# Attention in a fused transformer block: the last batch's additional maxima spread over steps, the first biases written into later steps, and the first batches' halves in another ring

## The chip, the cores and the metric

The kernel runs on one core of a Trainium2 chip. The metric is the device time of one execution in microseconds (us). Matrix products run on TensorE (PE), with its weight loads shown as a row of their own (PEld); reductions and elementwise work run on VectorE (DVE), ScalarE (ACT) and GpSimd (POOL). Most transfers are issued from the queue of SyncE (SP).

## The reference, cut to what matters

The whole block is attention, a routed feed-forward, a gated linear attention with its own feed-forward, and the routed feed-forward again. Only the first part is touched by the change:

```python
q = split_heads(x @ Wq + bq)                 # x is layer-normed, 8 batches of 512 x 256
k = split_heads(x @ Wk + bk)                 # 16 heads of 16
v = split_heads(x @ Wv + bv)
scores = einsum('bhqd,bhkd->bhqk', q, k) * scale
sparsity = scores.max(axis=-1) - scores.mean(axis=-1)
_, top_idx = top_k(sparsity, U)              # U = 307 of 512 queries
...                                          # those queries get softmax(scores) @ v, the others 0
out = out.transpose(0, 2, 1, 3).reshape(b, l, D)
return out @ Wo + bo
```

So each score is needed twice: once for the row maxima, which choose the queries, and once for the exponentials. The kernel subtracts the mean of the keys first, so that a row's mean is zero, and computes the outputs of all queries; those that are not chosen are multiplied by zero at the end.

## The kernel before, in words

The attention stage walks over 128 steps, `steps = (b, m, e, k)`: eight batches, two chunks of eight heads (`m`), two interleaved sets of four heads (`e`), four tiles of 128 positions (`k`). One loop over `n` does two things in each round. For the step `ahead` it makes four row maxima, one for each head `j` (`max_one`): two products on a strip of 32 rows (L582), with the high and the low halves of the queries, and a DVE reduction (L588). For the step `here`, 16 rounds behind (`LAG`), it makes four exponentials (`exp_one`): three products (L608) and an ACT activation (L615). In a round the eight items go in two groups, each of two exponentials and two maxima, and `together` interleaves their products, so that four heads' products stand side by side in four strips of the array. After each group PE multiplies the exponentials of the round before with the values (`weigh`, L630).

PSUM banks: exponentials take one of three banks of `bank`; maxima take one of the four of `bank_m`, which also holds the projections of the fronts and the transposed maxima (`mxT_ps`). A bank comes free when DVE or ACT has read it.

The fronts. `front(b, ...)` makes a batch's queries, keys and values in small pieces. In a round of the first 14 (`FIRST`) the pieces of batches 0 and 1 are drawn from `pieces`; later fronts run one piece a round, from round 21 (`LEAD`) on, for the batch two ahead. `halves` splits a projection into a high half (ACT, L446) and a low one (ACT at L452 and a POOL subtraction at L453; for the very first chunk a DVE operation at L448). Both lie in tiles of the tag `half`, a ring of four, until DMAs have moved them into `qh`, `ql` and `km` (L391). The tag `e` is a ring of ten for the exponentials and, earlier, for the scratch tile of `sum_stats`.

`place_maxima` runs some rounds after a group of maxima is complete (the list `full` has the round): POOL copies the maxima into `apart` (L548), PE transposes them (L554), ACT writes the two tiles `top` (L558, L562), also of the tag `half`, a DMA puts the whole ones into `neg` (L561), and POOL or, for the last batch, DVE makes `tops` (L566, L570 and L571), which the exponentials read as a third operand. When the last maxima are placed, `top_queries` runs 26 rounds of `max` and `match_replace` on DVE (L659, L662) over `neg`; `weights_of` then makes the weights (L147, L148), and `weigh_outputs` starts the end of the stage (L161, L164).

The additional maxima. From round 112 on, each fourth round also makes the maxima of one more step, all four at once, after the round's two groups:

```python
all_maxima(ahead)
if n >= 112 and n % 4 == 0 and coming < len(steps):
    ahead = steps[coming]
    together([max_one(*ahead, i, bank_m) for i in range(4)])
    all_maxima(ahead)
```

This happens in rounds 112, 116 and 120, and the last maxima are done in round 124, not 127.

`add_bias(b)` adds the output bias to a batch of the residual `xres` on POOL (L398); it is called for batches 0 to 2 in round 11.

The tile framework orders the instructions of each engine when the program is built, by priority and by when it reckons that operands are ready; the text's order is followed mostly, not always. Buffers of a tag are waited for by semaphores.

## Time and profile before

| | us |
|---|---|
| median of 3 runs | 1603.43 |
| lowest, highest | 1598.21, 1610.94 |
| profiled execution, its time | 1599.7 |
| its span, first to last instruction | 1598.0 |
| mean granted TensorE clock in it | 0.98 |

Busy time and its share of the span: PE 1547.5 us (97%), weight loads 860.5 (54%), DVE 943.9 (59%), ACT 704.5 (44%), POOL 454.5 (28%). The attention stage is the first third: step 16's exponentials begin at 71.7 us, step 112's at 443.6, step 143's end at 551.1, and the weights of the outputs are done at 552.6. Matmuls are pipelined and their ends are modelled, so that a busy PE need not be a fast one. A row of the timeline is: start, duration, engine, line, operation, output and input, shapes, number, and in brackets how long the engine had been idle and what ended that.

### The profile page before, as it was taken

The page shows a single profiled execution, that of the slowest core. Times are in us where ns is not written, and L with a number is a line of the kernel's source. Part 1 is how long each engine was busy: PE and PEld are TensorE (multiplying, and loading weights), DVE is VectorE, ACT ScalarE, POOL GpSimd, SP SyncE. Part 2 cuts the span into 40 slices and gives each one's busy share as a digit, 9 for nine tenths or more (in the row PEclk, how much of TensorE's full clock was granted, in tenths as well). Part 3 has the DMA queues.
Part 4 walks back from the last instruction along what each step waited for, and adds up shares of the span by engine and source line. Part 5 has one row for each costly group of instructions (what it writes and reads, how often), then busy time and mean ns, then how long its engine had stood idle before and what let it go on. Part 6 is the DMA issues. An engine that isn't in the chain of part 4 may idle for free.

```text
span 1598.0 us, 21558 instructions
## 1 busy us (share of the span) xinstructions
PE 1547.5 (97%) x7982; PEld 860.5 (54%) x7982; DVE 943.9 (59%) x1974; ACT 704.5 (44%) x1290; POOL 454.5 (28%) x547
## 2 busy tenths in 40 slices
PE   6799999999999999999999999999999999999999
PEld 3344444444444376655564556546545655767666
DVE  6688776776776974547744566467275532354332
ACT  4377777677765843442255225432631542221110
POOL 4653453452220241123433233234243210000000
PEclk9899999999996999999999999999999999999999
DMA  5301112112110051100000001000000010011100
GB/s 188 122 16 68 42 42 81 42 42 81 42 42 2 3 171 27 40 2 13 1 0 0 0 2 27 0 0 1 1 1 1 0 28 1 23 31 40 40 27 27
DMA packets 38553, 52.65 MB, mean 33 GB/s; under 512 B 9068, under 2 KB 22580, under 8 KB 38448
## 3 DMA queue, kind: packets, MB, share of 16 engines
q1 hardware_dynamic: 37648, 50.09, 9.6%
q8 instruction: 63, 1.03, 0.3%
q10 hardware_dynamic: 800, 1.18, 0.2%
q14 instruction: 42, 0.34, 0.1%
HBM read 21.24 MB, written 4.33 MB: 16 GB/s over the span
## 4 chain that ended last, share of the span: by engine, by line
PE 78%; DVE 11%; ACT 4%; POOL 4%; issue 2%; DMA 2%; SPq 0%; ACTq 0%; POOLq 0%; DVEq 0%
PE y_ps L1087 17%; PE h_ps L1113 11%; PE s L608 10%; PE av L630 8%; PE swi_ps L1140 8%; PE proj_ps L1226 7%; PE s L582 5%; DVE pr L1259 2%; PE v_ps L505 2%; DVE pr L1249 2%; PE gla_y L1356 2%; PE q_ps L435 2%; PE k_ps L435 2%; POOL o L1276 1%; PE chT_ps L944 1%
## 5 line engine op out<-in xcount | busy, mean ns | idle before, releaser
L588 DVE TENSOR_REDUCE mx<-s 128x1 f32<-128x512 f32 x512 | 325.8, 684 | 119.2 <-PE s L582 118.1
L615 ACT ACTIVATE e<-s 128x512 f32<-128x512 f32 x512 | 276.0, 600 | 127.5 <-PE s L608 121.1
L1087 PE MATMUL y_ps<-w,h 128*128 128x256 f32 x1024 | 236.6, 387 | 8.2 <-DVE h L1122 7.6
L1113 PE MATMUL h_ps<-xnT,w 128*128 128x512 f32 x512 | 228.2, 594 | 0.0
L1087 PEld LDWEIGHTS y_ps<-w,h 128*128 128x128 f32 x1024 | 194.8, 193 | 48.8 <-DVE h L1122 13.2
L1113 PEld LDWEIGHTS h_ps<-xnT,w 128*128 128x128 f32 x512 | 94.7, 190 | 105.8 <-issue 103.8
L630 PE MATMUL av<-e,va 128*32 128x512 f32 (+1 forms) x1216 | 148.7, 559 | 2.1 <-ACT st L640 2.0
L582 PE MATMUL s<-km,qh 32*128 32x512 f32 x512 | 137.5, 508 | 8.5 <-DMA km<-half 4.4
L1121 ACT ACTIVATE h<-h_ps,b 128x512 f32<-128x512 f32 x96 | 65.3, 685 | 176.7 <-PE h_ps L1113 176.7
L1122 DVE TENSOR_TENSOR h<-h,mk 128x512 f32<-128x512 f32 x128 | 94.1, 749 | 82.7 <-ACT h L1121 62.0
L608 PE MATMUL s<-qh,km 32*128 32x512 f32 x512 | 139.4, 508 | 0.9 <-ACT e L615 0.8
L1098 DVE TENSOR_TENSOR xres<-xres,y_ps 128x512 f32<-128x512 f32 x47 | 32.2, 685 | 155.1 <-PE y_ps L1087 117.9
L1140 PE MATMUL swi_ps<-zT,w_up 128*128 128x512 f32 x256 | 122.4, 597 | 0.3 <-DVE h L1149 0.3
L1140 PE MATMUL swi_ps<-zT,w_gate 128*128 128x512 f32 x256 | 121.6, 593 | 0.0
L1087 PE MATMUL y_ps<-w_down,h 128*128 128x256 f32 x512 | 117.5, 380 | 0.0
L1226 PE MATMUL proj_ps<-q_w,rT 128*128 128x512 f32 x256 | 115.3, 594 | 0.5 <-ACT al L1209 0.4
L608 PE MATMUL s<-ql,km 32*128 32x512 f32 x512 | 112.9, 408 | 0.0
L608 PE MATMUL s<-tops,takes 4*128 4x512 f32 x512 | 110.3, 402 | 0.0
L582 PE MATMUL s<-km,ql 32*128 32x512 f32 x512 | 110.2, 412 | 0.0
L582 PEld LDWEIGHTS s<-km,qh 32*128 32x128 f32 x512 | 55.5, 187 | 101.5 <-DVE mx L588 68.4
L1087 PEld LDWEIGHTS y_ps<-w_down,h 128*128 128x128 f32 x512 | 95.1, 190 | 19.0 <-issue 7.4
L1146 ACT ACTIVATE h<-swi_ps 128x512 f32<-128x512 f32 x64 | 38.1, 595 | 139.9 <-PE swi_ps L1140 139.7
(235 smaller groups left out, 2186.9 us busy)
## 6 DMA issues: line engine op xcount, KB each, us to landing
mk<-md SPq DMA_DIRECT2D x32, 256.0 KB
qh<-half SPq DMA_DIRECT2D x63, 128.0 KB
ql<-half SPq DMA_DIRECT2D x63, 128.0 KB
km<-half SPq DMA_DIRECT2D x63, 128.0 KB
out<-xres SPq DMA_DIRECT2D x15, 256.0 KB
xres<-in_L_attn_a_x SPq DMA_DIRECT2D x7, 512.0 KB
w<-in_f_w1T SPq DMA_DIRECT2D x1, 1024.0 KB
w<-in_f_w2T SPq DMA_DIRECT2D x1, 1024.0 KB
```

The source lines that it names most:

```text
L435: nc.tensor.matmul(ps, w[:, c, bass.ts(m, P)], x[:, c, :], start=(c == 0), stop=(c == NC2 - 1),)
L582: nc.tensor.matmul(s, (qh, ql)[i].bitcast(HALF)[rows, e, bass.ts(k, P)], km.bitcast(HALF)[rows, e, :], start=(i == 0), stop=(i == 1),)
L588: nc.vector.tensor_reduce(mx[:, b % 2, m, e, r : r + 1], s, AX.X, ALU.max)
L608: nc.tensor.matmul(s, keys.bitcast(HALF), queries.bitcast(HALF), start=(i == 0), stop=(i == 2),)
L615: nc.scalar.activation(ex, s, AF.Exp, scale=1.0 / DH**0.5)
L630: nc.tensor.matmul(av[32 * j : 32 * j + 32, queries], va[:, 8 * kt + 4 * m + j, DH * e : DH * e + 2 * DH], es[j][:, queries], start=(kt == ...
L1087: nc.tensor.matmul(y[0][:, bass.ts(i, D)], h[f][:, bass.ts(2 * u + i, P)], w[:, f, :], start=(f == 0), stop=(f == NF - 1),)
L1113: nc.tensor.matmul(ps, w1[:, c, bass.ts(f, P)], xT[g][:, c, :], start=(c == 0), stop=(c == NC2 - 1),)
L1121: nc.scalar.activation(hf, ps, AF.Relu, bias=b1[:, f : f + 1])
L1122: nc.vector.tensor_tensor(hf, hf, mk[g][:, f, :], ALU.mult)
L1140: nc.tensor.matmul(ps, w[:, c, bass.ts(f, P)], zT[g][:, c, :], start=(c == 0), stop=(c == NC2 - 1),)
L1226: nc.tensor.matmul(ps, rT[b // G4][:, c, bass.ts(b % G4, P)], q_w[:, c, m], start=(c == 0), stop=(c == NC2 - 1),)
```

## The change

It does three things.

1. The additional maxima of the last batch are no longer made four at once in rounds 112, 116 and 120. They are put into a list, `extra`, and made one a round, and two a round from 120 on, after the round's groups. The books (`all_maxima`) are kept as before, in the same rounds; the placing of batch 7's maxima of chunk 0 goes one round later.
2. `add_bias` for batches 0, 1 and 2 is called in rounds 18, 22 and 26, not three times in round 11.
3. The halves of batches 0 and 1 and the first pair of `top` tiles are taken from the ring `e` of ten, not from the ring `half` of four.

```diff
+            def half_tile(first, name):
+
+                tag, bufs = ("e", 10) if first else ("half", 4)
+                return a2.tile([P, L], F32, tag=tag, name=name, bufs=bufs)
+
@@ halves
-                    hi, lo = (
-                        a2.tile([P, L], F32, tag="half", name=f"half{b}", bufs=4)
-                        for i in range(2)
-                    )
+                    hi, lo = (half_tile(alone, f"half{b}") for i in range(2))
@@ place_maxima
-                whole, hi = (
-                    a2.tile([P, L], F32, tag="half", name=f"top{b}", bufs=4) for i in range(2)
-                )
+                whole, hi = (half_tile(b + m == 0, f"top{b}") for i in range(2))
@@ all_maxima
             coming = 0
+            extra = []
...
-                    full.append((n + 2, (b, m, (0, 1))))
+                    full.append((n + 2 + b // (NB - 1), (b, m, (0, 1))))
@@ the loop
-                    all_maxima(ahead)
-                    if n >= 112 and n % 4 == 0 and coming < len(steps):
-                        ahead = steps[coming]
-                        together([max_one(*ahead, i, bank_m) for i in range(4)])
+                    if n >= 112 and n % 4 == 0 and coming + 1 < len(steps):
+                        extra = [(*steps[coming + 1], i) for i in range(4)]
                         all_maxima(ahead)
+                        all_maxima(steps[coming])
+                    else:
+                        all_maxima(ahead)
+
+                    for _ in range(2 if n >= 120 else 1):
+                        if extra:
+                            together([max_one(*extra.pop(0), bank_m)])
...
-                    if n == 11:
-                        for b in range(3):
-                            add_bias(b)
...
+                    if n in (18, 22, 26):
+                        add_bias((n - 18) // 4)
```

In the built program DVE, ACT and SP keep their order but for the placing of batch 7's first maxima (a few places later); PE's order changes from round 112 on. On POOL, the first `tops` come between the normalizing operations of batch 2, the low half of batch 1's last keys comes ahead of the bias additions, and these, written into rounds 18 to 26, stand in POOL's order around the values' biases of batch 1: two before the first pair, one before the second, and all three ahead of the `apart` copy of round 17.

## The prediction

> **What bounds the kernel now.** I read the page first: TensorE (PE) is busy 97% of the span, so time is lost where PE stands still or where its clock is cut. The slices show both places (slices of 40 us; the third row is the granted clock).

> ```profile
> PE 1547.5 (97%) x7982; PEld 860.5 (54%) x7982; DVE 943.9 (59%) x1974; ACT 704.5 (44%) x1290; POOL 454.5 (28%) x547
> ...
> PE   6799999999999999999999999999999999999999
> ...
> PEclk9899999999996999999999999999999999999999
> ```

> The first two slices are thinly filled, and slice 13 (480 to 520 us) has six tenths of the clock. Both are in the attention stage, the first 553 us, which the change touches. Next I read the table of stages. A step's edges are the starts of its first exponential (L615, four to a step). Columns: PE, weight loads, DVE, ACT, POOL busy, clock, DMA.

> ```profile
> 381.46:385.62 4.16, 4.16 (x34) 1.49 (x37) 2.99 (x5) 3.84 (x8) 0.51 (x1) 1.00 0.01 4
> ...
> 443.59:449.87 6.28, 5.60 (x42) 2.11 (x45) 5.14 (x9) 4.00 (x8) 2.12 (x3) 1.00 0.00 1
> ...
> 477.14:483.22 6.08, 5.32 (x45) 2.26 (x44) 5.48 (x10) 2.65 (x5) 0.77 (x1) 0.94 0.01 3
> ...
> 495.44:500.63 5.19, 5.19 (x40) 2.08 (x44) 2.58 (x5) 2.17 (x4) 0.20 (x1) 0.50 0.00 0
> ```

> Step 96 takes 4.16 us; step 112, with the same pieces of a front and a burst of four additional maxima, takes 6.28 and leaves PE idle for 0.68. Step 120, the third burst, takes 6.08, idles 0.76, and the clock falls in it. Step 123 runs wholly at half clock: 5.19 where step 100, equal in work, takes 3.08. The timeline shows what PE waits for in a burst: a free bank, that is, a DVE reduction (L588).

> ```profile
> 465.42 0.18 PEld L582 LDWEIGHTS s<-km,qh 32*128 32x128 f32 x1 [0.99 <-DVE mx L588]
> 465.42 0.50 PE L582 MATMUL s<-km,qh 32*128 32x512 f32 x1 [0.55 <-DVE mx L588]
> ```

> Then the end of the stage: DVE starts the top-k rounds at 508.27, when the last row of maxima has landed, and is busy without a break until the weights at 551.93; the last exponentials end at 551.1. The two chains are level, and DVE's is the last.

> ```profile
> 508.27 0.43 DVE L656 COPY work<-neg 128x512 f32<-128x512 f32 x1 [1.23 <-DMA neg<-top]
> ...
> 547.85 3.35 DVE L147 RECIPROCAL neg<-den 128x512 f32<-128x512 f32 x1
> ...
> 551.93 0.69 DVE L148 SCALAR_TENSOR_TENSOR nrm<-work,neg 128x512 f32<-128x512 f32 x1
> ```

> Last, the timeline of the start. The halves of batch 1's second chunk (ACT L446) wait 5.77 us for POOL's `tops`, since all share four buffers; PE starts no matmul between 55.2 and 60.13; and POOL holds three bias adds (6.98 us) ahead of the next half and of the `apart` copy that step 17's transposes need.

> ```profile
> 57.52 1.26 POOL L571 TENSOR_TENSOR tops<-top,top 128x512 fp32r<-128x512 f32 x1
> ...
> 58.81 0.69 ACT L446 ACTIVATE half<-q_ps,bq 128x512 fp32r<-128x512 f32 x1 [5.77 <-POOL tops L571]
> ...
> 61.95 6.98 POOL L398 TENSOR_TENSOR xres<-xres,bo 128x1024 f32<-128x1024 f32 x3
> ...
> 73.14 0.21 POOL L548 COPY apart<-mx 128x32 f32<-128x32 f32 x1 [0.23 <-DVE mx L588]
> ```

> **The clock, as this trace has it.** Half-clock stretches last 6.8 us (59.2 to 66.1), 6.8 (72.9 to 79.7) and 30.7 (482.5 to 513.2), all multiples of 3.41. I weighed each matmul record by columns, by its share of 128 rows and of 128 columns, and doubled those of plain f32 (`av`, `q_ps`, `v_ps`, ...), which follow each other at twice the distance of the halves'. In the 3.41 us before each fall the sum is 0 to 2048; no stretch of 3072 or more is followed by one; it returned to full after 3072 to 3136 and more, while 1600 to 3104 left it at half. So about 3000 in 3.41 us is the level. A full step weighs 1088 (exps) + 1024 (maxima) + 2048 (`av`) = 4160.

> **Part 1, the late maxima.** Same instructions, other places: twelve maxima go from three bursts (steps 112, 116, 120) to lone ones, one a step in 112 to 119 and two in 120 and 121. The placing of the last batch's first maxima goes from step 119 to 120; its `tops` are first read in step 128, eight steps later, so this costs nothing.
> - Removed. Without bursts, at full clock, steps 112 to 123 would take what the same places took elsewhere: 4.16 + 4.09 + 4.17 + 3.09 + 3.09 (steps 96, 97, 50, 99, 100), then 3.1 each for seven and 0.6 more for two with transposes (step 119's 3.77): 41.5. The trace has 443.59 to 500.63 = 57.0. So 15.5 goes: some 8 in bursts, 7.4 at half clock.
> - Added. A lone maximum has two products in one row group that follow each other. Four together take 0.34 (first product) + 0.23 (second); a lone one takes as long, less what the next group, on other rows, runs beside its second product. Bounds: 0.23 (the first alone shows) and 0.7 (a whole group's share, weights and all); I take 0.5, nearer to the group. Twelve make 6.0 (2.8 to 8.4). DVE does five reductions in 3.0 us of a 3.6 us step and six in 3.6 of 4.1: it keeps up.
> - Step 124 to the top-k start: 7.64 at half clock, some 6.5 at full: 1.1 saved.
> - Does the clock hold? A step with one lone maximum weighs 4416 in 3.6 us, which is 4180 in 3.41; with two, 4672 in 4.1 us, 3890. Both are over 3000.
> [...] No run here shows a lone one yet.
> Sum: 15.5 - 6.0 + 1.1 = 10.6 earlier for DVE's top-k chain, which then carries the end alone, 43.5 us from its start. The exps (19 steps at 2.2 from step 125) now end some 4 us ahead of it, so PE stands for 4 us before the `nrm_ps` products (L161). That is below the level, so the clock falls there and the products of L161 and L174 run partly at half: 0 to 5, I take 2.5.

> **Parts 2 and 3, the start.** The halves of batches 0 and 1 and the first tops get the exps' ring of ten, which nobody uses before step 16. ACT's wait of 5.77 goes, and so does an earlier one: the tops at 51.14 and 52.45 held a bank that PE waited 1.07 for. Then step 13's maxima, at 65.10 now (DVE idle 6.58), come at about 57.5, right behind step 12's, and all follows 7.6 earlier. But POOL: in the built program the three adds, though written in steps 18, 22 and 26, still stand ahead of step 17's `apart`; only the key half (L453) now goes before them. From 53.71 to that copy POOL has 2.18 + 1.57 + 1.26 + 1.26 + 0.21 + 1.26 + 0.42 + 6.98 + 2.79 = 17.9 and gaps: `apart` at 71.8. PE would be there by 70.9; it did the transposes at 78.48. So 6.6 is gained there, not 7.6. Behind the transposes in PE's queue stand the second group of step 17 and all later exps, so the whole chain waits. The `tops` of step 16's exps are ready by 57.6, and the ring's buffers of batch 1's second chunk, whose key transfers were issued at 65.2 to 72.6 before and come earlier now, are needed by step 18 only: no cost.
> Then the clock. Steps 14 and 15 are maxima alone, 1024 in 2.5 us, so it falls there as before, and the wait for POOL keeps it low. A window at half costs 3.41 x (1 - 3.08/5.19) = 1.4. Before, it returned at 79.72 on 3088, a near thing. I take two windows beyond step 17: -2.8, giving 3.8. Bounds: 7.6 (no cap by POOL, no window) and -4.6 (eight windows, till batch 2's dense front pieces, which start in step 21, lift the sum).

> **Sum** against the profiled execution (1599.7, span 1598.0, 1.7 around it): 10.6 - 2.5 + 3.8 = 11.9, so 1587.8. This execution is 3.7 below the median, 1603.43, and 1.5 above the lowest; I give the number as it stands. Faster by over 1% means below 1587.4; 1% is about what a measurement of this kernel can tell from no change.

> **Rivals.**
> - A: the clock comes back at once in step 17 and PE's stand before L161 costs nothing: 1599.7 - 10.6 - 6.6 = 1582.5. For it: the return at 79.7 after two windows. Against it: nine windows at half from 482.5 with PE busy for 30.39 of 30.70. [...]
> - B: the late half clock comes all the same, from the two-a-step steps: 15.5 - 7.4 - 6.0 = 2.1, with PE not ahead at the end, and 3.8: 1593.8. For it: that stage is where it fell. Against: 3890 is well over the level.
> - C, slower: the half clock of steps 14 to 17 holds on. Each bare step costs 5.19 - 3.08 = 2.1 more. The 14.7 of the other gains is used up from seven such steps; held through step 37, twenty steps, it costs 42: 1627. For it: full steps gave 2592 to 3104 and did not end it late; against: no front pieces there, and from step 21 each adds to the sum.
> - D: the change does not do what it says: adds still ahead, lone maxima at 0.7, the exps' ring held up by a late DMA: 1600.

> **How the numbers follow.** Forecast 0.50 (its own range 1581 to 1595, half of it below 1587.4), A 0.20, B 0.13, C 0.09, D 0.08. Faster 0.25 + 0.20 + 0.02 from B = 0.47; slower 0.08, C but for its shorter forms; same 0.45. The range: A with the cheapest lone maxima (3.2 less) and some of POOL's cap gone is 1578; up to D and the short forms of C, 1602.

> **What would show it.** Right: no step of 6 us at 112, 116, 120; no half clock from 482 on; the top-k copy (L656) some 14 us earlier; PE idle just before L161; ACT's L446 without a wait for `tops`; step 13's reductions right behind step 12's; PE waiting for `apart` in step 17. Wrong: steps 112 to 121 as long as before, a half-clock stretch over three windows after step 17, or L656 less than 8 us earlier.

## The result, and the profile after

The changed kernel took 1588.57 us in the median of 6 executions (1585.32 to 1594.44), beside 1605.2 of the kernel before: a ratio of 0.990 [0.986, 0.994]. Twelve more executions in a later measurement gave 1594.51 (1587.21 to 1599.63) beside 1603.83, a ratio of 0.994 [0.991, 0.997]; the median of all 18 is 1590.0. Ratios, here and below, leave out the four executions that took over 1.5% more than the fastest of their kernel (three of before, one of part 2 alone); medians do not. The forecast was 1587.8. The profiled execution took 1585.32 (span 1583.6), 14.4 less than the profiled one of before.

First the page of the changed kernel: the engines, then TensorE's 40 slices and the granted clock. The 6 that the clock had in slice 13 is gone; an 8 now stands in slice 14, at the hand-over from the exps to the outputs.

```profile
PE 1536.1 (97%) x7982; PEld 858.6 (54%) x7982; DVE 942.4 (60%) x1974; ACT 703.6 (44%) x1290; POOL 454.0 (29%) x547
...
PE   6899999999999899999899999999999999999999
...
PEclk9899999999999899999999999999999999999999
```

**The late steps.** The table by stage of the changed kernel, steps 112, 120 and 124 (columns: window, length, busy time and count of PE, PEld, DVE, ACT and POOL, granted clock, DMA share, GB/s):

```profile
440.78:445.15 4.37, 4.37 (x36) 1.68 (x39) 3.60 (x6) 3.88 (x8) 0.71 (x1) 1.00 0.01 2
...
471.30:476.51 5.21, 4.81 (x48) 2.22 (x44) 4.19 (x8) 3.63 (x8) 0.21 (x1) 1.00 0.02 6
...
487.40:492.87 5.47, 4.54 (x47) 2.21 (x50) 3.25 (x6) 3.96 (x10) 1.09 (x3) 1.00 0.02 6
```

Step 112 is 4.37 long where it was 6.28, PE is never idle in it, and the clock is 1.00 throughout; the half clock of 30.7 us from 482.5 is not there. From step 112 to step 124 it is 46.62 us where it was 57.04. Step 120, though, is 5.21 with 0.40 of PE idle, and step 124 has 0.93.

The timelines of the top-k chain and of the hand-over behind it, DVE and then PE:

```profile
494.04 0.43 DVE L656 COPY work<-neg 128x512 f32<-128x512 f32 x1 [1.24 <-DMA neg<-top]
...
537.71 0.69 DVE L148 SCALAR_TENSOR_TENSOR nrm<-work,neg 128x512 f32<-128x512 f32 x1
...
538.45 4.92 PE L161 MATMUL nrm_ps<-nrm,spread 32*128 32x512 f32 x16 [3.29 <-DVE nrm L148]
543.30 6.35 PE L174 MATMUL ao_ps<-wo_a,outC 128*128 128x256 f32 x16
```

The chain starts 14.2 us earlier (508.27 before), and `nrm` as much. PE now stands 3.29 us before L161, the clock falls at 538.4 for 10.2 us, and the products of L161 take 4.92 where they took 3.03, those of L174 6.35 where they took 3.72. The first addition of `ao` to the residual (POOL, L181) is 10.7 earlier, not 14.2. The 3.5 lost here came back in later stages, which drew less half clock in this execution: from `nrm` to the end it is 1046.1 before and 1045.9 after.

**The start.** Lines of the timeline up to step 17, after the change (line numbers are those of the changed kernel: what was L446 is L448 here, L398 is L403, L548 is L550, L554 is L556):

```profile
51.70 0.69 ACT L448 ACTIVATE half<-q_ps,bq 128x512 fp32r<-128x512 f32 x1 [1.12 <-PE q_ps L440]
...
53.37 14.54 DVE L588 TENSOR_REDUCE mx<-s 128x1 f32<-128x512 f32 x24
...
62.58 4.66 POOL L403 TENSOR_TENSOR xres<-xres,bo 128x1024 f32<-128x1024 f32 x2
...
68.57 2.36 POOL L403 TENSOR_TENSOR xres<-xres,bo 128x1024 f32<-128x1024 f32 x1
...
72.23 0.22 POOL L550 COPY apart<-mx 128x32 f32<-128x32 f32 x1
...
72.50 1.12 PE L556 MATMUL mxT_ps<-ident,apart 128*128 128x128 f32 x4 [1.40 <-POOL apart L550]
```

ACT's halves wait for their projection and no longer for `tops`; DVE makes 24 reductions in a row where it stood 6.58 us; step 16 starts at 64.20 instead of 71.74. The three adds (L403) are still ahead of `apart`, and PE waits for it. Step 17 takes 8.39 us, at half clock (64.0 to 81.1), and step 20 starts at 85.20 instead of 88.43: of 7.5 us, 3.2 are left.

### The profile page after: what moved, and what is told of

Same layout as the page of the kernel before. It is cut to its first block, busy times and chain, and to the rows that moved or that the text cites. A ratio compares the mean times of both kernels' runs of the same rounds, so it can differ in the third digit from the quotient of the medians.

```text
span 1583.6 us, 21546 instructions
## 1 busy us (share of the span) xinstructions
PE 1536.1 (97%) x7982; PEld 858.6 (54%) x7982; DVE 942.4 (60%) x1974; ACT 703.6 (44%) x1290; POOL 454.0 (29%) x547
## 4 chain that ended last, share of the span: by engine, by line
PE 74%; DVE 11%; POOL 5%; ACT 4%; issue 3%; DMA 2%; SPq 0%; POOLq 0%; DVEq 0%; ACTq 0%
PE y_ps L1092 16%; PE h_ps L1118 10%; PE s L608 9%; PE swi_ps L1145 8%; PE av L630 7%; PE proj_ps L1231 7%; PE s L582 4%; DVE pr L1264 2%; PE q_ps L440 2%; POOL o L1281 2%; DVE pr L1254 2%; PE k_ps L440 2%; PE gla_y L1361 2%; PE v_ps L507 2%; DVE w L1256 2%
## 5 line engine op out<-in xcount | busy, mean ns | idle before, releaser
L588 DVE TENSOR_REDUCE mx<-s 128x1 f32<-128x512 f32 x512 | 325.3, 684 | 108.8 <-PE s L582 107.7
L615 ACT ACTIVATE e<-s 128x512 f32<-128x512 f32 x512 | 275.9, 600 | 119.5 <-PE s L608 115.0
L1092 PE MATMUL y_ps<-w,h 128*128 128x256 f32 x1024 | 232.9, 383 | 8.7 <-DVE h L1127 8.1
L630 PE MATMUL av<-e,va 128*32 128x512 f32 (+1 forms) x1216 | 144.4, 543 | 2.0 <-ACT st L640 2.0
L582 PE MATMUL s<-km,qh 32*128 32x512 f32 x512 | 135.6, 501 | 5.8 <-DMA km<-half 4.1
L582 PE MATMUL s<-km,ql 32*128 32x512 f32 x512 | 109.5, 404 | 0.0
L582 PEld LDWEIGHTS s<-km,qh 32*128 32x128 f32 x512 | 54.4, 184 | 96.1 <-DVE mx L588 64.4
```

The source lines that it names most:

```text
L582: nc.tensor.matmul(s, (qh, ql)[i].bitcast(HALF)[rows, e, bass.ts(k, P)], km.bitcast(HALF)[rows, e, :], start=(i == 0), stop=(i == 1),)
L588: nc.vector.tensor_reduce(mx[:, b % 2, m, e, r : r + 1], s, AX.X, ALU.max)
L615: nc.scalar.activation(ex, s, AF.Exp, scale=1.0 / DH**0.5)
L630: nc.tensor.matmul(av[32 * j : 32 * j + 32, queries], va[:, 8 * kt + 4 * m + j, DH * e : DH * e + 2 * DH], es[j][:, queries], start=(kt == ...
L1092: nc.tensor.matmul(y[0][:, bass.ts(i, D)], h[f][:, bass.ts(2 * u + i, P)], w[:, f, :], start=(f == 0), stop=(f == NF - 1),)
```

## How far single executions differ, and why

So each kernel can be split into what it costs at equal half-clock time and how much of that time it draws (+- is one standard error):

| kernel | executions | median us | half clock, mean us | at equal half clock, against before |
|---|---|---|---|---|
| before | 56 | 1603.64 | 72.2 +- 2.6 | 0 |
| changed | 18 | 1590.0 | 61.1 +- 2.6 | -7.4 +- 0.5 |
| part 1 alone | 10 | 1595.31 | 55.8 +- 2.7 | -2.8 +- 0.7 |
| part 3 alone | 10 | 1603.83 | 84.6 +- 5.7 | -4.2 +- 0.7 |
| part 2 alone | 10 | 1603.75 | 71.2 +- 6.0 | +0.7 +- 0.7 |
| parts 2 and 3 | 10 | 1603.05 | 83.9 +- 4.1 | -4.7 +- 0.7 |
| late fillers | 10 | 1607.09 | 70.4 +- 3.6 | +5.6 +- 0.7 |
| changed, bias fetched later | 10 | 1591.01 | 61.7 +- 3.8 | -8.0 +- 0.7 |
| changed, products at the hand-over | 10 | 1591.47 | 59.5 +- 3.0 | -6.7 +- 0.7 |
| changed, later bias, start fillers | 4 | 1581.16 | 36.4 +- 3.8 | -7.4 +- 1.1 |
| that, and `tops` on POOL | 6 | 1583.93 | 38.5 +- 3.8 | -7.6 +- 0.9 |
| parts 2 and 3, later bias, start fillers | 12 | 1590.41 | 49.3 +- 3.2 | -4.7 +- 0.7 |

The changed kernel's 11.3 us (means: 1601.1 and 1589.9 of span) are 7.4 at equal clock and 11.1 x 0.348 = 3.9 of clock. The 2.8 of part 1 and the 4.7 of parts 2 and 3 make 7.5, so the parts add up.

The row of before has the 56 executions of two measurements; 23 more, made beside the last one, and the six beside the first are not in it. With the 23 the slope is 0.345, and every figure of the last column is 0.3 to 0.5 lower. With a constant for each measurement's chip as well, the figures move by up to 1.4 (the last row becomes -6.1, the changed kernel -8.5). The +- of the last column are those of the fit alone and leave this out.

## The experiments

The first four build on the kernel before.

**Part 1 alone** (`e1_late`).

```
-                    full.append((n + 2, (b, m, (0, 1))))
+                    full.append((n + 2 + b // (NB - 1), (b, m, (0, 1))))
...
+                    for _ in range(2 if n >= 120 else 1):
+                        if extra:
+                            together([max_one(*extra.pop(0), bank_m)])
```

> The kernel before with part 1 alone: lone maxima in place of the three bursts. Theory (the late part is most of the gain, and most of it is the half clock of steps 120 to 126 that no longer comes): step 112 to the top-k copy (L656) takes 53 to 54 us where before took 64.7, no half-clock stretch begins between steps 112 and 126, PE stands for 3 us before L161 and the clock falls there, some 4 us given back; the time is 7 us (4 to 11) under the kernel before, ratio 0.9956. Rival (the gain is in the start, the late part only moves a wait): L656 less than 4 us earlier counted from step 112, time within 2 us of before.

Measured: 1595.31, ratio 0.996 [0.993, 0.999], 7.9 under the kernel before in the medians. Steps 112 to 123 take 46.62 as in the changed kernel, and L656 comes 53.24 after step 112 (64.68 before), as expected. PE stands 3.30 before L161, but the clock falls there for one window only, and 1.2 is given back (the `ao` add comes 7.81 after `nrm`, 6.59 before), not 4. In means of the span the gain is 8.5, and the table above divides it: the smaller part is bursts that are gone (2.8), the larger the clock (72.2 to 55.8 us of half clock, 5.7). That the bursts draw half clock is seen in the profiles as well: in steps 112 to 123 the clock fell in four of the six that have bursts, and in one of the seven that have lone maxima. What the prediction did not have is a fall of the clock after step 98, behind ACT's wait for a buffer of `half`. ACT's timeline there, PE's, and the window at half clock in the table by stage:

```profile
398.58 0.69 ACT L452 ACTIVATE half<-k_ps,bk 128x512 f32<-128x512 f32 x1 [0.88 <-DMA neg<-top]
...
399.32 0.50 PE L582 MATMUL s<-km,qh 32*128 32x512 f32 x1 [0.52 <-ACT half L452]
...
401.50:415.20 13.70, 13.70 (x86) 5.37 (x82) 7.17 (x13) 6.73 (x14) 0.98 (x2) 0.50 0.06 21
```

ACT waits 0.88 us for a buffer that a DMA of `neg` still reads (`top`, of the same ring); PE stands for half a microsecond, and the clock then stays at half for 13.7 us with PE busy all the time, which cost 5.9 (steps 96 to 111 took 68.0 instead of 62.1). The same fall is in two more of the profiles, of part 2 alone and of the late fillers, and not in the others.

The wait alone does not decide it. The changed kernel's first profile has the same wait of PE, and its clock stayed full:

```profile
391.85 0.50 PE L582 MATMUL s<-km,qh 32*128 32x512 f32 x1 [0.52 <-ACT half L454]
```

The load of the window that holds the wait differs: by the prediction's measure, with each matmul record shared out over the windows that it spans, it is 2740, 2800 and 2740 in the three profiles with the fall, and 3480 and 3030 in the changed kernel's two profiles, where PE waits 0.52 and 0.40 and the clock holds. From these five sums it seems to matter where the edges of the windows lie beside the wait. That was not tried by itself, but it would make the time of one kernel differ between executions.

**Part 3 alone** (`e2_ring`).

```
-                    hi, lo = (
-                        a2.tile([P, L], F32, tag="half", name=f"half{b}", bufs=4)
-                        for i in range(2)
-                    )
+                    hi, lo = (half_tile(alone, f"half{b}") for i in range(2))
...
+                whole, hi = (half_tile(b + m == 0, f"top{b}") for i in range(2))
```

> The kernel before with part 3 alone: halves of batches 0 and 1 and the first tops in the ring of the exps. Theory (this part carries the whole gain of the start): ACT's wait of 5.8 us for tops is gone, step 16's first exponential is some 7.5 us earlier, then the wait for POOL's apart copy in step 17 and the half clock of steps 14 to 18 give a part back: 2 to 6 us earlier from step 20 on, and the late part as before. Time 4 us (1 to 7) under before. Rival (part 2 is what frees POOL): without it the bias additions stand ahead of the last key half and of apart as before, and step 16 is less than 4 us earlier.

Measured: 1603.83, ratio 1.002 [0.998, 1.007]. Step 16 starts at 64.4, 7.3 earlier, as expected; but the clock is at half from 64.2 for 27.3 us, and step 24 is 0.7 later than before. The expected time was missed; the table has the reason: 4.2 us gained at equal clock, 12 us more half clock.

**Part 2 alone** (`e3_bias`): `add_bias` for batches 0 to 2 written in steps 18, 22 and 26 instead of 11.

> The kernel before with part 2 alone: add_bias of batches 0 to 2 written into steps 18, 22 and 26. Theory: in the built program the additions still stand ahead of step 17's apart copy, and what they no longer hold up (the last low half of batch 1's keys) is first read in step 24: step 20 within 0.7 us of before, time within 2 us of before (ratio 0.999 to 1.001). Rival (POOL's queue is what bounds the start): step 20 more than 2 us earlier.

Measured: 1603.75, ratio 1.000 [0.996, 1.004], as expected: part 2 alone does nothing that can be measured. The profile is of use for another thing: in this execution the clock did not fall late, and steps 112 to 123, bursts and all, took 49.9. So of the 57.0 in the profile of before, 7.1 was half clock, and bursts cost 49.9 - 41.5 = 8.4 at full clock.

**Fillers in the late steps** (`e4_fill120`): two products with a zero weight tile, added to `av`, in the first halves of steps 120 and 121.

```
+                        if half == 0 and n in (120, 121):
+                            for _ in range(2):
+                                nc.tensor.matmul(
+                                    av, none, wv.rearrange("p c m -> p (c m)"),
+                                    start=False, stop=False,
+                                )
```

> The kernel before, all bursts kept, with two products of zero weights (128x128, 512 columns, plain f32, 0.85 us each, added to av, which they leave as it is) in the first half of steps 120 and of 121: 3.4 us of PE work more. Theory (the late loss of before is mostly the clock, which follows the load of PE's array, not the stalls): the load in the windows round the third burst stays over the level, the clock doesn't fall before step 124, steps 121 to 126 take 22 us in place of 31, and L656 is 5 to 8 us earlier in spite of the work added; the time is 2 to 6 us under before. Rival (DVE's backlog is the loss, the clock only follows it): L656 no earlier than before, and the time 1 to 3 us over before.

Measured: 1607.09, ratio 1.005 [1.002, 1.008], 3.9 over in the medians. The theory's time was missed; the rival's 1 to 3 over is nearer, but below what came. The clock did not fall at 482 but at 491.8, still ahead of step 124, for 6.8 us. L656 is at 514.88, later than before; counted from step 112 it is 1.6 earlier (63.08 instead of 64.68). At equal half clock the kernel with the fillers costs 5.6 more. Part 2 alone, with bursts and no fillers, had no fall there at all, so one profile each does not settle between the theory and its rival.

The next three build on the changed kernel.

**The output bias fetched later** (`e5_bo`), so that POOL's adds must come behind `apart`.

```
-                    if n == 9:
+                    if n == 16:
                         nc.gpsimd.tensor_copy(bo[0:1, 0:1], maximum_of(n))
                         nc.sync.dma_start(out=bo, in_=t["L0_attn_a_bo"].partition_broadcast(P))
```

> The changed kernel with one edit: the output bias is fetched in step 16 instead of step 9, so that GpSimd's three bias adds (4.66 and 2.32 us in the profile after the change) stand behind the copy `apart` that step 17's transposes wait for. Theory (GpSimd caps the start): PE's wait of 1.4 us for `apart` in step 17 goes, `mxT_ps` comes about 1.5 us earlier than 72.5, and the late steps' start (L656) with it if the clock stays where it was: time 1 to 2 us under the changed kernel's. Rival (the clock sets the start): the wait goes, but the steps 14 to 18 are at half clock all the same, the late start is within 0.5 us of 494.0, and the time is that of the changed kernel.

Measured: 1591.01, ratio 0.993 [0.990, 0.996]. POOL's and PE's timelines:

```profile
66.74 0.21 POOL L550 COPY apart<-mx 128x32 f32<-128x32 f32 x1 [0.34 <-DVE mx L588]
...
72.19 1.12 PE L556 MATMUL mxT_ps<-ident,apart 128*128 128x128 f32 x4
```

`apart` is ready 5.2 us ahead, PE no longer waits for it, and step 17 takes 6.92 instead of 8.39, as expected. The time is that of the changed kernel all the same: the clock is at half from 64.8 for 30.7 us, and step 20 starts at 87.7. The rival's time came; its late start did not (L656 is 9.1 later than 494.0), since more half clock lies ahead of it: 30.7 us after step 16 instead of 17.1, and 10.2 us from step 120 on. At equal half clock the kernel stands at -8.0 +- 0.7 beside the changed kernel's -7.4 +- 0.5: POOL's cap is real, but what it costs is too small to be seen.

**Products at the hand-over** (`e6_hand`), to keep the array loaded while PE stands before L161.

```
+            warm = bank("warm")
+            for i in range(3):
+                nc.tensor.matmul(warm, ident, last_es[i], start=True, stop=True)
```

> The changed kernel with three plain f32 products added (an identity by the last exps' tiles, into a bank that nobody reads) between the last weighted sum and the `nrm_ps` products, to hold TensorE's clock in the 3.3 us in which PE stands for `nrm`. Theory (PE's stand costs the clock there, 10.2 us of half clock from 538.4): no half-clock stretch begins at the stand; the 16 products of L161 take about 3.0 us instead of 4.9 and those of L174 about 3.7 instead of 6.35; the first GpSimd add of `ao` comes 6 to 8 us after `nrm` (L148) instead of 10.1; time 3 to 4.5 us under the changed kernel's. Rival: the clock falls all the same or the chain there is paced by another engine, and the add still comes 9 to 11 us after `nrm`: no gain.

Measured: 1591.47, ratio 0.993 [0.990, 0.996]. In its profile L161 and L174 take 3.03 and 3.72 and the `ao` add comes 6.7 after `nrm`, as expected of it: the products fill 2.84 us of the stand, and the clock holds. But no time follows. The later profile of the changed kernel itself shows why (below): the long stand is not in every execution. The clock fell at the hand-over in the four profiles in which PE stands 3.29 or 3.30 there, and in none of the eight others without these products, in which it stands 0.4 to 2.1.

**Fillers in the start** (`e7_start`): the later bias and, in steps 14 to 16, one product with a zero weight tile each.

```
+                    if n <= LAG:
+                        nc.vector.tensor_copy(warm_w[0:1, 0:1], maximum_of(n - 1))
+                        nc.tensor.matmul(
+                            acc("warm"), warm_w, wv.rearrange("p c m -> p (c m)"),
+                            start=True, stop=True,
+                        )
```

> As the kernel with the later output bias, and beside it one plain f32 product with a zero weight tile, into a scratch bank, in each of the steps up to 16 (it waits for that step's predecessor's maxima), so that the steps of maxima alone (14 to 16) load TensorE's array more. Theory (the load of the array in each 3.41 us sets the clock, some 3000 keeping it): 1024 of maxima and 1024 of filler in 2.5 us are some 2800 in 3.41 us, so the clock either stays full or falls for one window only; steps 17 to 19 then take about 3.1 to 4.2 each and step 20 starts at 81 to 83 instead of 85.2: time 2 to 4 us under the changed kernel's. Rival (the clock falls at a fixed place whatever PE does, or the fillers cost what they save): step 20 at 84 to 87, time within 1 us of the changed kernel's or above it.

**Parts 2 and 3 on the kernel before** (`e11_start`).

> The kernel before with the parts 2 and 3 alone (bias adds in later steps, first halves in the ring of the exps); the late maxima as before. Theory (the start parts give a gain that the clock takes back in part): step 16 starts about 7.5 us earlier than 71.7, step 20 between 3 and 4 us earlier than 88.4, as in the changed kernel, and the time is 3 to 4 us under the kernel before. Rival 1 (together they do no more than the ring alone): step 20 at 88, time within 1 us of the kernel before. Rival 2 (the parts give all 7 us): step 20 at 81 to 82, 6 to 7 us under.

Measured: 1581.16, ratio 0.988 [0.982, 0.994], with the fillers (4 executions), where 2 to 4 under the changed kernel was expected and 8.8 came; and 1603.05, ratio 1.000 [0.996, 1.003], for the two parts alone, where 3 to 4 under the kernel before was expected and nothing came, as rival 1 had it. In that profile step 16 starts 3.6 earlier than before and not 7.5, with 10.2 us more of half clock in the first 50 us, and step 20 at 91.4. The table by stage of the two parts alone, steps 17, 18 and 19:

```profile
72.45:80.66 8.21, 6.68 (x33) 3.08 (x32) 3.83 (x11) 3.26 (x7) 5.73 (x6) 0.50 0.01 2
80.66:86.17 5.51, 5.51 (x41) 2.18 (x44) 3.15 (x8) 2.17 (x4) 1.17 (x5) 0.50 0.00 0
86.17:91.36 5.19, 5.19 (x40) 2.08 (x44) 3.21 (x8) 2.17 (x5) 2.31 (x12) 0.50 0.01 3
```

and of the changed kernel with fillers, the same steps:

```profile
71.17:75.25 4.08, 4.03 (x32) 1.82 (x32) 3.37 (x8) 3.15 (x6) 1.51 (x1) 1.00 0.10 36
75.25:78.36 3.11, 3.11 (x37) 1.55 (x36) 3.06 (x7) 2.17 (x4) 3.11 (x2) 1.00 0.00 1
78.36:81.52 3.16, 3.16 (x37) 1.48 (x36) 3.09 (x8) 2.18 (x5) 3.16 (x3) 1.00 0.03 5
```

The third column from the end tells it: clock 0.50 beside 1.00, with PE busy for the whole of steps 18 and 19 in both. With three products of about 1.1 us before step 17 the clock is 1.00 from 60 to 92 us, and the three steps take 10.35 us instead of 18.91. The run that differs from the one with fillers by the fillers alone is that with the later bias: there the three steps take 17.63, the median is 9.85 higher and the half clock 61.7 us instead of 36.4, at the same cost at equal half clock within the uncertainty (-8.0 and -7.4). In profiles, the stretch at half clock after step 16 is in all six that have part 3 and no fillers, and in none of the three with fillers. In the changed kernel's first profile the window ahead of the fall at 64.0 weighs some 1830 by the prediction's measure, records shared out, and the four behind it that were followed by another at half weigh 1610 to 2540. A worked reason, argued from the prediction's measure and not tried by itself: a bare step of exps and maxima weighs 4160; in 3.41 us that is 4160 x 3.41 / 3.08 = 4600 at full clock, but 4160 x 3.41 / 5.19 = 2730 at half, below the about 3000 that the prediction took from the trace of before. So the half clock would hold itself until denser steps come (the front's pieces from step 21 on), or until a window happens to hold more than its share.

**The changed kernel once more** (`again_after`), the same text.

> The changed kernel itself once more, for a second profile and more executions. So far the time of an execution follows its time at half clock (span against half-clock time over nine kernels: 0.34 us per us). Theory: the median is 1586 to 1592 with some 55 to 60 us of half clock; in its profile the stretch after step 16 is 17 to 31 us long, and the hand-over before L161 (PE stands some 3 us) brings a half-clock stretch in some executions only: the first GpSimd add of `ao` comes 6.7 us after `nrm` where it does not, about 10 where it does. Rival (the first profile is typical): the same stretches as before, 17.1 at 64 and 10.2 at 538.

Measured: 1594.51, ratio 0.994 [0.991, 0.997], 2.5 us above the expected range, with 64 us of half clock where 55 to 60 were expected. The half clock after step 16 lasts 30.7 us here, step 20 starts at 90.2, 1.8 later than before (with 10.2 us more of half clock in the first 50 us), and another stretch of 6.8 us lies at step 124. PE's timeline at the hand-over:

```profile
545.88 3.03 PE L161 MATMUL nrm_ps<-nrm,spread 32*128 32x512 f32 x16 [0.60 <-DVE nrm L148]
548.97 3.72 PE L174 MATMUL ao_ps<-wo_a,outC 128*128 128x256 f32 x16
```

The stand is 0.60 and costs nothing: the half clock at step 124 made the exps later by about what the top-k chain is behind. The stand of 3.29 in the first profile is one of several forms.

**`tops` of the last batch on POOL** (`e12_pool`), beside the start fillers.

```
-                if b == NB - 1:
+                if b == NB - 1 and len(es) * len(tiles) < 4:
```

> The kernel with the three start fillers and the later output bias, and beside them one edit: the `tops` of the last batch's first chunk and of the second chunk's first tiles are made on GpSimd, as for the other batches, and not on VectorE (L566, 0.75 us each and 1.0 of waiting for ACT's copy in DVE's queue, with the reductions behind it). Theory (in steps 120 to 124 DVE is behind, which the prediction denied): step 120 shrinks from 5.2 to some 4.0 to 4.5 and steps 120 to 124 by 1.0 to 2.0 together, PE's idle time of 0.4 and 0.93 there goes in part; 1 to 2 us at equal half-clock time. Rival (PE sets these steps): the sum of steps 120 to 124 changes by less than 0.4, and the time is that of the kernel with fillers, 1579 to 1584.

Measured: 1583.93, ratio 0.988 [0.984, 0.993]. Step 120 shrinks from 5.21 to 4.03, but step 122 grows from 3.85 to 4.40, since PE now waits 0.72 for `apart`, behind the copies on POOL. Steps 120 to 124 take 21.09 instead of 21.58: between the two expectations, and not to be seen in the time.

**Start fillers without part 1** (`e14_startfill`): parts 2 and 3, the later bias and the fillers, bursts as before.

> The kernel before with parts 2 and 3 (which alone gave 0.9998 of the time before), the output bias fetched in step 16, and the three zero-weight fillers in steps 14 to 16; the late maxima as before. Theory (the parts 2 and 3 give some 5 us, and the half clock that they lengthen after step 16 takes them back): the stretch after step 16 is gone or one window long, step 20 starts at 81 to 82 instead of 88.4, the half-clock time falls by 15 to 25 us against the 84 of the parts alone, and the time is 1590 to 1597, 6 to 13 under the kernel before. Rival (the fillers helped only beside part 1, or by chance): time within 3 us of 1603.

Measured: 1590.41, ratio 0.990 [0.987, 0.994], where parts 2 and 3 alone gave 1603.05. Step 20 starts at 79.9, and no half clock lies between 24 and 327 us; the table by stage has clock 1.00 for the whole of it:

```profile
23.70:327.30 303.60, 297.05 (x2368) 130.85 (x2365) 234.02 (x446) 210.57 (x420) 144.12 (x192) 1.00 0.20 69
```

The half clock falls from 83.9 to 49.3, 34.6 us (15 to 25 were expected), which at 0.348 is 12.0; at equal half clock both stand at -4.7. The theory's time came, and the division holds without part 1 too: the start parts are worth some 5 us at equal clock, and what they lose is clock. That the two figures agree to a tenth is chance; with a constant for each chip they are -5.0 and -6.1.

The two versions with fillers and part 1 beat both kernels: 1581.16 (4 executions) and 1583.93 (6 executions).

## Why the prediction was right, point by point

- **Baseline and bursts: right.** Forecast 41.5 + 6.0 = 47.5 for steps 112 to 123; measured 46.62. Bursts 8 (8.4 by part 2's profile), half clock 7.4 (7.1).
- **Lone maxima: right side of the estimate, cheaper.** Steps 112 to 119 sum to 2.56 us above their bare lengths, 0.32 each for eight, not 0.5; the bounds were 0.23 and 0.7.
- **"It keeps up": wrong.** DVE falls behind in steps 120 to 124, where the last batch's `tops` wait for ACT in DVE's queue. The changed kernel's DVE timeline:

```profile
482.94 0.75 DVE L566 SCALAR_TENSOR_TENSOR tops<-top,less_odd,top 128x512 fp32r<-128x512 f32 x1 [1.06 <-ACT top L562]
483.61 4.87 DVE L588 TENSOR_REDUCE mx<-s 128x1 f32<-128x512 f32 x8
```

  Eight reductions have piled up behind one wait of 1.06. Counting DVE's reductions by step left the waits in its queue out; with these `tops` on POOL, step 120 shrinks by 1.2. The cheaper lone maxima paid for it.
- **Late sum 10.6 earlier: right for that execution** (from step 112 to L656 it took 53.26 instead of 64.68, 11.4 less). By its terms it is 2.1 of work (8.1 of bursts less 6.0) and 8.5 of half clock (7.4 and 1.1). Part 1 alone gave 2.8 +- 0.7 at equal half clock and 16.4 x 0.348 = 5.7 of clock. The term that was mis-sized is the clock's: it stood in the sum as if every execution had the late fall, and two of the six profiles with bursts have none in steps 112 to 123.
- **The hand-over, 2.5 (0 to 5): in the first profile about 3.5 (the `ao` add), in the second 0, with part 1 alone 1.2.** The forecast lies between what occurs.
- **The start: 7.6 right, POOL's cap right, the clock mis-sized.** Step 16 came 7.5 earlier; among the four profiles without fillers that have 13.6 us of half clock in the first 50 us, it comes 7.8 to 10.4 earlier in the three with part 3. `apart` was at 72.23 (forecast 71.8). The cap's price of 1.0 is not to be seen, as the later bias shows. "Two windows beyond step 17" fitted the first profile in its sum (step 20 3.2 earlier, forecast 3.8) and not in its parts: step 17 itself took 2.6 more than before, where the prediction had 1.0, and little more than one window lies behind it, which cost 1.7. The return "on 3088, a near thing" was no near thing: that sum leaves out four products that start at 79.53, and with them the window has 3584, or 3250 with records shared out at its edges. In the five other profiles with part 3 and without fillers the stretch lasts 27.3 to 30.7 us, and four to five windows of it lie behind step 17; it ends in step 20 or 21, with the front pieces of batch 2, where the prediction's lower bound let it end. Five windows at 1.4 are 7.0, so the whole term is about 0 in those profiles, not 3.8. That the first profile showed the forecast's figure is luck.
- **The rivals.** A (the clock back at once) is what the fillers make; the changed kernel does not do it. B, the late half clock all the same, came in one of the seven profiles with part 1 (with the later bias, in step 120) and in neither of the changed kernel's own. C's course, a half clock that holds on through bare steps with PE busy (5.51 and 5.19 us for steps 18 and 19 of parts 2 and 3 alone), is in the traces; it ended in step 20 or 21 and not at step 37. D fell, but for the adds that stand ahead of `apart`, as the forecast itself had them.
- **The signs.** Those named for a right forecast were all there in the first profile: no step of 6 us at 112, 116 or 120, L656 14.2 earlier, PE standing before L161, no wait for `tops` at L448, PE waiting for `apart`. One named for a wrong one, a stretch of over three windows behind step 17, is in the second.
- **The total: right, in part by luck.** The sum had 2.1 + 6.6 = 8.7 of work and 8.5 - 2.5 - 2.8 = 3.2 of clock; over all executions it was 7.4 +- 0.5 and 11.1 x 0.348 = 3.9, with some 1.3 of uncertainty. So both halves agree, but the single clock terms were off on both sides (late 5.7 for 8.5, hand-over less than 2.5, start -4.1 for -2.8) and nearly cancel: luck. So is the time itself: the sum started from an execution of 1599.7, and the first measurement had before at 1605.2, so that 16.6 were gained there and not 11.9; in the later one it was 9.3. The parts' clock terms, 5.7 and -4.1, add up to 1.6 and not 3.9; with the scatter of the half-clock means (about +-2 us of time for the four together) that difference is not shown to be more than chance.

## What to carry to other kernels

Read the granted clock of every execution before the time: where it differs between executions, as here (36.4 to 84.6 us of half clock in the means, 0.348 us of time for each), split each comparison into its part at equal half-clock time and its part of clock, or a real gain shows as nothing, as the 4.7 us of parts 2 and 3 did (1603.05 beside 1603.64). A change that fills an idle stretch early can lose the gain again in the steps behind it: here steps 17 to 19 took 18.91 us at half clock and 10.35 at full, and three spare products ahead of them cost less than the half clock that they spared. And a sum for an engine needs the waits in its queue, not the busy time alone: here DVE stood 1.06 us before L566, with eight reductions behind it.

## What the runs showed of the hardware that was not expected

- The half clock held for 54.6 us (from 467.0, part 3 alone), with PE busy for 53.6 of them. The table by stage, step 118 there:

```profile
473.55:479.11 5.56, 5.56 (x41) 2.17 (x44) 2.63 (x5) 2.17 (x4) 0.00 (x0) 0.50 0.00 0
```

- The same sum on either side: a window of 2910 (from 77.6, records shared out) let the clock return in the changed kernel, and one of 2920 (from 83.7) did not in the kernel of parts 2 and 3. In these traces the measure from the matmul records gives a level near 3000, not the moment of a change.
- Products with zero weights were enough for the clock: with three of them, 1.10 to 1.13 us each, the 17.1 to 30.7 us of half clock after step 16 are gone.
- A wait of half a microsecond on PE (step 98) cost 5.9, or nothing: with 0.52 us of it the clock fell in one profile and held in another.
